# A three-layer graph network on one core: who shares a PSUM bank with whom, and two more blocks of layer 1 by count matrices

## The chip, the cores and the metric

The kernel runs on one core of a Trainium2 chip. Its time is the device time of one launch in microseconds (us), here the median of several runs. The core has five engines with a queue of their own each: TensorE (PE, matrix products, with its weight loads shown as PEld), VectorE (DVE), ScalarE (ACT), GpSimd (POOL) and SyncE (SP, which only issues DMAs here). POOL issues the indirect gathers. Matrix products land in PSUM, which this kernel uses as eight banks of 128 rows by 512 fp32 numbers.

## The reference

`x` has 6250 rows of 256; 100,000 edges `(src, dst)` come sorted by `dst`, and every node has an edge to itself besides. With `dinv = 1/sqrt(degree)`, each of three layers computes

```python
h = h @ W                                     # 256->512, 512->512, 512->256
msg = h[src] * (dinv[src] * dinv[dst])[:, None]
h = relu(segment_sum(msg, dst, n) + b)
```

and the result is `layernorm(x + h)`. The kernel sums neighbours first and multiplies by `W` afterwards in the first two layers, and multiplies by `W3` at the end of layer 2, so that the summed rows are 256, 512 and 256 wide.

## The kernel before

The nodes are 50 blocks of Q = 125 rows. A block's sum over its edges is made in one of two ways.

*Gathered.* The block's edges lie in 16 chunks of 128 places. `gather` (L965) has POOL fetch 128 rows by index into one row buffer of a ring (tiles `room` and `spare`). `more_hots` (L934, DVE) compares column numbers with the edges' destinations and so makes four one-hot matrices `shot`. `product` (L991, PE) multiplies one-hot by rows and adds up in a bank `sacc`. fp32 rows take two passes; most chunks are split first into a high half (L1006, ACT) and a low half (L1009, DVE) in one fp32r tile `halves`, which goes at one pass per half. Chunks of layer 1 are split every other time, those of layer 2 seven times out of eight.

*By a count matrix.* `counts` (L697) makes, for 125 destinations, a matrix of how often each of the 6250 sources occurs: 25 products of one-hot matrices per block (L728, PE, 250 columns each), whose one-hots `hot_lo`, `hot_key` DVE makes by comparison (L705), and which ACT copies as bytes into an SBUF buffer (L737). The matrix is stored to DRAM (`kept`) and fetched back by `fetch`. The sum is then 50 dense products (L1034) with `parts`, the whole table in SBUF, after `converted` (L942, ACT) has turned bytes into fp32r, five products per piece. No gather is needed.

Layer 1 (`layer(0, ...)`) treats blocks 0 to 17 (FEW = 18) by count matrices and gathers 32. Layer 2 is 512 wide: it gathers 44 blocks, and `teams` (L763) does six, three at a time, by streaming the table past stored counts (products L814, one block's share every PACE = 2 chunks) into three further banks. Layer 2 also makes ten further count matrices, one at a time (`alone`). Layer 3 uses all 28 (MANY) and gathers 22.

The order is fixed when the program is built. `layer` walks over the gathered chunks; for each chunk it issues the gather, the splits of earlier chunks, the product of the chunk `lag` = 4 earlier, then the steps of finished blocks (`go`) and the steps of the extras (`go_fixed`): windows, counts, teams. The steps are Python generators that yield the number of chunks to wait (SOON = 2, LATE = 6). All engines work through their queues in that order; semaphores do the rest. `take` and `free` count the holders of a named bank or buffer. In `need`, if no sum bank is free when a block begins, the steps of finished blocks are run without spacing until one is; `late` counts these.

After a block: `after1` scales, transposes into bank `str` (L1057), multiplies by W1 in `smm` (L1081) and stores the rows of table 1. `after2` fetches the block's own rows of table 1 (a row of the gather ring is borrowed for it), waits LATE chunks, adds them (L1102, DVE), gives the sum bank back, scales (L1104, ACT), transposes into `str`, copies out (L1112), and for every two blocks (a couple) multiplies by W2 (L1125) and W3 (L1142), both in bank `win_ps`, and stores table 2.

The eight banks: `near_cols`, three `sacc`, `smm`, `str`, `mat_ps`, `win_ps`. `near_cols` holds the column numbers that every comparison of DVE reads, in its first 250 columns; its other half is the third place for count products in layer 1 (two more lie in `mat_ps`) and the only place in layer 2:

```python
mat_places = [mat_ps[:Q, 0, :G * NB], mat_ps[:Q, 1, :G * NB], near[:Q, 256:256 + G * NB]]
mat_place = mat_places[2 if alone else m % 3]
```

Instructions of different engines on one bank are kept in order by semaphores in this program, whichever columns they touch, and reads against reads as well: before the change, 104 of the copies L737 out of `near_cols` wait for DVE alone.

Of the kernel before, what the change touches and what calls it, by code (L numbers as in the profile page):

```python
# [9 lines left out]
F32 = mybir.dt.float32  # L10
# [11 lines left out]
P = 128  # L22
# [3 lines left out]
Q = 125  # L26
KF = 16
# [13 lines left out]
FEW = 18  # L41
# [5 lines left out]
G = 5  # L47
# [334 lines left out]
def sorted_path(ctx: ExitStack, tc: tile.TileContext, x, edges, starts, found, wts, biases, room, late, out):  # L382
# [43 lines left out]
    mat_ps = ps_mat.tile([P, 2, 256], F32, name="mat_ps")  # L426
# [5 lines left out]
    scratch = w2_sb.rearrange("p k n -> p (k n)")  # L432


    def windows(t):
# [55 lines left out]
        sl_ps = ps_mat.tile([P, 512], F32, name="win_ps")  # L491
# [3 lines left out]
        nc.scalar.copy(slots[:, t], sl_ps.rearrange("p (t v) -> p t v", t=2)[:, :, :Q])  # L495
        yield SOON
# [190 lines left out]
    mat_places = [mat_ps[:Q, 0, :G * NB], mat_ps[:Q, 1, :G * NB], near[:Q, 256:256 + G * NB]]  # L687
# [3 lines left out]
    tr_bank = ps_sum.tile([P, KH, Q], F32, name="str")  # L691
    mat_bank = mat_ps.rearrange("p t n -> p (t n)")
    win_bank = ps_mat.tile([P, HID], F32, name="win_ps")
    idle = {}


    def counts(blocks, places, rush=0, alone=False):  # L697
# [12 lines left out]
        for s in range(total + 5):  # L710
# [10 lines left out]
            if s < total and s % WIDE == 2:  # L721
                t, w = divmod(blocks[s // GB] * GB + s % GB + 1, Q)
                compared(hot[s // WIDE][1][:, 3:], slots[:, t, 1, w:w + WIDE - 3])
            m = s - 4
            if 0 <= m < total:
                hot_lo, hot_key = [h[:, m % WIDE] for h in hot[m // WIDE]]
                mat_place = mat_places[2 if alone else m % 3]
                nc.tensor.matmul(mat_place, lhsT=hot_lo, rhs=hot_key, start=True, stop=True)  # L728
            if alone:
                yield 1  # L730
            else:
                m = s - 5
            if 0 <= m < total:
                n, u = divmod(m, GB)
                place = places[n % len(places)]
                mat_place = mat_places[2 if alone else m % 3]
                nc.scalar.copy(place[:, :, u * G:(u + 1) * G], mat_place.rearrange("p (k r) -> p k r", r=G))  # L737
                if u == GB - 1:
                    by_rows(nc.sync, place.rearrange("p k v -> p (k v)"), kept[blocks[n]], store=True)
                    stored.append(blocks[n])  # L740
            if s >= rush or s % 2:
                yield 1
# [20 lines left out]
    def teams(groups):  # L763
# [35 lines left out]
        for u, (g, k) in enumerate(units):  # L799
# [4 lines left out]
            for n, b in enumerate(groups[g]):  # L804
# [14 lines left out]
                yield PACE  # L819
# [35 lines left out]
    held = {}  # L855

    def free(name, bank=None):
        held[name] -= 1
        if name in idle:
            idle[name].append(bank)  # L860

    team_ended = [None]

    def take(name, most):
        while held.get(name, 0) >= most:
            yield 1
        held[name] = held.get(name, 0) + 1

    def layer(i, width, gathered, dense, after, rows, first=0, spacing=1.0, extras=()):
# [98 lines left out]
        def product(c):  # L968
# [83 lines left out]
    def transposed(z, width, got):  # L1052

        yield from take("tr", 1)
        zt_ps = tr_bank
# [37 lines left out]
    def after2(b, acc, bank):  # L1093
# [19 lines left out]
        free("tr")  # L1113
# [4 lines left out]
        yield soon  # L1118
        yield from take("ht2", 1)
        for f2 in range(0, KH, 2):  # L1120
# [14 lines left out]
            if not f2:  # L1135
                yield soon
# [91 lines left out]
    split = two.enter_context(tc.tile_pool(name="swide_split", bufs=4))  # L1228
    groups = [every[g * TEAM:(g + 1) * TEAM] for g in range(TEAMS)]
# [3 lines left out]
          + [(10 + gap * n, counts([b], (made,), alone=True)) for n, b in enumerate(many[FEW:])])  # L1233
# [190 lines left out]
```

## Time and profile before

| | us |
|---|---|
| median of 3 runs (lowest, highest) | 2312.32 (2309.65, 2316.81) |
| the profiled execution, its own time | 2304.01 |
| its span, first to last instruction | 2302.3 |
| before the first gather | 98 |
| layer 1 to the first gather of layer 2 | 98 to 795 |
| layer 2 to the first gather of layer 3 | 795 to 1832 |
| layer 3 | 1832 to 2302 |

The page gives busy shares per engine over the span; as the three layers have different limits, the times are read by layer. A line of the groups reads: line, engine, operation, output and inputs, shapes, count, busy us, mean ns of one, then the idle time of that engine just before these instructions and what ended it. Waits name who waited for whom, the total, how often, and the longest. In the timeline a matmul's duration includes its way through the array; the distance from one start to the next is what it costs when they come back to back.

### The profile page before, as it was taken

How to read it: one execution, taken by the hardware profiler on the slowest of the kernel's cores; microseconds unless marked ns; L12 is line 12 of the kernel's file. 1: busy time of each engine (PE TensorE's matmuls, PEld its weight loads, DVE VectorE, ACT ScalarE, POOL GpSimd, SP SyncE). 2: the span in 40 equal slices, each digit the busy share in tenths (PEclk: the TensorE clock that was granted, in tenths of full speed). 3: DMA queues.
4: the chain of work that ended last, by engine and by line, in shares of the span. 5: the costliest groups of instructions: out<-in, count | busy, mean ns of one | idle time of the engine just before them, and what ended most of it. 6: DMA issues, size and time to landing. Idle time of an engine off the chain costs nothing.

```text
span 2302.3 us, 30500 instructions
## 1 busy us (share of the span) xinstructions
PE 1977.0 (86%) x8361; PEld 1447.2 (63%) x8361; DVE 1588.9 (69%) x3021; ACT 1340.3 (58%) x2957; POOL 1600.0 (69%) x1620
## 2 busy tenths in 40 slices
PE   3378889899889778989898898899988699999997
PEld 2256666566566445666666666666766577777775
DVE  5677767667664387877776777777777267777776
ACT  1456666656665365766665666566655255555564
POOL 2277677777767577777776777677777177777776
PEclk9989999999999889999999999999999999999998
DMA  8455555665555788888899787888798256667664
GB/s 176 115 146 154 163 168 163 177 182 159 169 164 151 202 246 245 256 261 251 231 256 271 225 266 218 245 234 244 227 276 234 65 162 185 171 183 188 184 175 130
DMA packets 188446, 455.76 MB, mean 198 GB/s; under 512 B 43725, under 2 KB 78682, under 8 KB 188263
## 3 DMA queue, kind: packets, MB, share of 16 engines
q0 software_dynamic: 99776, 301.07, 46.2%
q1 hardware_dynamic: 73367, 140.87, 21.8%
q10 hardware_dynamic: 15120, 11.77, 2.1%
q8 instruction: 67, 1.10, 0.2%
q14 instruction: 116, 0.95, 0.1%
HBM read 399.68 MB, written 53.88 MB: 197 GB/s over the span
## 4 chain that ended last, share of the span: by engine, by line
PE 50%; DVE 16%; DMA 14%; issue 9%; ACT 7%; POOL 2%; ACTq 0%; DVEq 0%; POOLq 0%; SPq 0%
PE sacc L991 16%; DMA room<-tab,ssrc 7%; PE sacc L1034 6%; PE win_ps L1125 4%; DMA spare<-tab,ssrc 4%; PE smm L1034 4%; PE mat_ps L1034 4%; DVE hot_key L705 4%; PE smm L1081 4%; PE win_ps L1034 4%; DVE halves L1009 3%; PE win_ps L1142 2%; ACT halves L1006 2%; DVE shot L934 2%; PE near_cols L728 2%
## 5 line engine op out<-in xcount | busy, mean ns | idle before, releaser
L965 POOL DMA_INDIRECT room<-tab,ssrc x971 | 975.5, 1005 | 329.4 <-issue 144.1
L965 POOL DMA_INDIRECT spare<-tab,ssrc x597 | 589.8, 988 | 198.7 <-issue 85.9
L991 PE MATMUL sacc<-halves,shot 128*125 128x512 f32 x1840 | 685.6, 439 | 24.0 <-DVE halves L1009 20.3
L1009 DVE TENSOR_TENSOR halves<-room,halves 128x512 fp32r<-128x512 f32 (+1 forms) x771 | 430.0, 566 | 254.2 <-ACT halves L1006 250.1
L1006 ACT CAST halves<-room 128x512 fp32r<-128x512 f32 (+1 forms) x771 | 390.0, 520 | 195.1 <-PE sacc L991 86.3
L991 PEld LDWEIGHTS sacc<-halves,shot 128*125 128x125 f32 x1840 | 334.9, 192 | 171.3 <-issue 58.9
L934 DVE TENSOR_TENSOR shot<-near_cols,sdlo 128x500 fp32r<-128x500 f32 x417 | 280.3, 673 | 108.9 <-PE near_cols L728 60.3
L1009 DVE TENSOR_TENSOR halves<-spare,halves 128x256 fp32r<-128x256 f32 (+1 forms) x453 | 241.1, 540 | 149.3 <-ACT halves L1006 143.5
L1034 PE MATMUL sacc<-parts,piece 125*125 125x512 f32 x900 | 333.7, 446 | 3.7 <-ACT piece L942 3.7
L737 ACT CAST room<-near_cols 125x250 uint8<-125x250 f32 x400 | 175.0, 438 | 250.7 <-PE near_cols L728 97.9
L942 ACT CAST piece<-room 125x625 fp32r<-125x625 uint8 x376 | 267.9, 713 | 41.3 <-DVE piece L942 12.4
L1006 ACT CAST halves<-spare 128x256 fp32r<-128x256 f32 (+1 forms) x453 | 222.5, 501 | 98.8 <-PE sacc L991 36.5
L991 PE MATMUL sacc<-room,shot 128*125 128x256 f32 (+1 forms) x596 | 233.5, 475 | 18.1 <-DMA room<-tab,ssrc 13.1
L705 DVE TENSOR_TENSOR hot_key<-near_cols,slots 128x750 bf16<-128x750 f32 (+1 forms) x280 | 223.9, 800 | 19.9 <-ACT room L737 14.6
L728 PE MATMUL near_cols<-hot_key,hot_lo 128*125 128x250 bf16 x400 | 114.6, 287 | 137.9 <-DVE hot_key L705 107.1
L1125 PE MATMUL win_ps<-room,w_sb 128*128 128x250 f32 x800 | 204.1, 380 | 15.8 <-DVE st L1155 11.6
L728 PEld LDWEIGHTS <-hot_lo 128*125 128x125 bf16 x700 | 97.5, 140 | 185.0 <-DVE hot_key L705 133.0
L737 ACT CAST room<-mat_ps 125x250 uint8<-125x250 f32 x300 | 125.5, 437 | 120.6 <-PE mat_ps L728 119.9
L1125 PEld LDWEIGHTS win_ps<-room,w_sb 128*128 128x128 f32 x800 | 152.7, 192 | 53.9 <-DVE st L1155 16.3
L1034 PEld LDWEIGHTS sacc<-parts,piece 125*125 125x125 f32 x900 | 142.1, 190 | 58.9 <-issue 30.5
L1034 PE MATMUL smm<-parts,piece 125*125 125x512 f32 x500 | 141.6, 402 | 5.8 <-ACT piece L942 5.7
L991 PEld LDWEIGHTS sacc<-room,shot 128*125 128x125 f32 x596 | 112.8, 196 | 49.2 <-DMA room<-tab,ssrc 14.0
(201 smaller groups left out, 2637.4 us busy)
## 6 DMA issues: line engine op xcount, KB each, us to landing
room<-kept SPq DMA_DIRECT2D x46, 683.6 KB
parts<-tab SPq DMA_DIRECT2D x55, 448.0 KB
kept<-room SPq DMA_DIRECT2D x28, 683.6 KB
tab<-st SPq DMA_DIRECT2D x71, 224.0 KB
room<-tab,ssrc POOLq DMA_INDIRECT x971
spare<-tab,ssrc POOLq DMA_INDIRECT x597
spare<-tab SPq DMA_DIRECT2D x40, 224.0 KB
out<-st ACTq DMA_DIRECT2D x50, 112.0 KB
```

The source lines that it names most:

```text
L705: nc.vector.tensor_tensor(out, near_cols[:, :shape[2]].unsqueeze(1).to_broadcast(shape), numbers.unsqueeze(2).to_broadcast(shape), op=ALU. ...
L728: nc.tensor.matmul(mat_place, lhsT=hot_lo, rhs=hot_key, start=True, stop=True)
L737: nc.scalar.copy(place[:, :, u * G:(u + 1) * G], mat_place.rearrange("p (k r) -> p k r", r=G))
L934: nc.vector.tensor_tensor(hot[:, :n], near_cols[:, :Q].unsqueeze(1).to_broadcast([P, n, Q]), dlo.rearrange("p b j -> p (b j)")[:, at:at + ...
L942: convert(piece, used[m % 2][:, c * PIECE:(c + 1) * PIECE, :])
L965: nc.gpsimd.indirect_dma_start(out=row, out_offset=None, in_=tables[i], in_offset=bass.IndirectOffsetOnAxis(ap=at, axis=0))
L991: nc.tensor.matmul(acc[:Q, :size], lhsT=hot, rhs=row[:, c0:c0 + size], start=(i == 1 and k == c0 == 0), stop=(k == KF and c0 + size == row ...
L1006: nc.scalar.copy(halves[:, :width], landed[chunk - hi_lag])
L1009: nc.vector.tensor_sub(halves[:, width:], landed.pop(chunk - lo_lag), halves[:, :width].bitcast(F32))
L1034: nc.tensor.matmul(acc_d[:Q], lhsT=got[done // PIECE][:, k % PIECE, :], rhs=parts[:, k], start=False, stop=(k == NB - 1))
L1081: nc.tensor.matmul(y_ps, lhsT=zt[:, k, :], rhs=w1_sb[:, k, :], start=(k == 0), stop=(k == KC - 1))
L1125: nc.tensor.matmul(h_ps[:, f, :], lhsT=w2_sb[:, k, (f2 + f) * P:(f2 + f + 1) * P], rhs=zt2[:, k, :], start=(k == 0), stop=(k == KH - 1))
```

## The change

- FEW is 20: layer 1 makes and uses 20 count matrices and gathers 30 blocks, so 483 gathers in place of 516; layer 2 makes eight count matrices instead of ten.
- `near_cols` is no place for count products any more. In layer 1 they go in pairs, two in the halves of one bank, to whichever of `mat_ps` and `win_ps` is free; in layer 2 to `str`. One copy takes both out, two steps later. The windows (which find the edges for the counts) now take and free `win_ps` explicitly.
- From the 26th product on, layer 1's counts run six products in five chunks.
- In layer 2 the own rows of gathered blocks have a tile `own_row` of their own, fetched five chunks before the block's last product; the add comes SOON chunks after it. The transposes go into the block's own sum bank, which is given back after they are copied out. A team's block waits until it can be the second of a couple, except towards the end.
- The teams run one step in four a chunk earlier.

```diff
-FEW = 18
+FEW = 20
-    mat_ps = ps_mat.tile([P, 2, 256], F32, name="mat_ps")
+    mat_bank = ps_mat.tile([P, HID], F32, name="mat_ps")
+    win_bank = ps_mat.tile([P, HID], F32, name="win_ps")
...
         for h in range(2):
+            yield from take("win", 1)
             c0, c1 = h * half, min(EC, (h + 1) * half)
-            row_ps = ps_mat.tile([P, 512], F32, name="win_ps")
+            row_ps = win_bank
...
+            free("win")
...
-    mat_places = [mat_ps[:Q, 0, :G * NB], mat_ps[:Q, 1, :G * NB], near[:Q, 256:256 + G * NB]]
-    tr_bank = ps_sum.tile([P, KH, Q], F32, name="str")
+    tr_bank = ps_sum.tile([P, HID], F32, name="str")
+    count_banks = {"mat": mat_bank, "win": win_bank, "tr": tr_bank}
-    def counts(blocks, places, rush=0, alone=False):
+    def counts(blocks, places, banks, rush=0):
...
+        def copied(now_on):
+            while full and full[0][0] <= now_on:
+                _, name, ms = full.pop(0)
+                n, u = divmod(ms[0], GB)
+                place = places[n % len(places)]
+                nc.scalar.copy(place[:, :, u * G:(u + len(ms)) * G].rearrange("p k (t r) -> p t k r", r=G),
+                               count_banks[name].rearrange("p (t v) -> p t v", t=2)[:Q, :len(ms), :NB * G]
+                               .rearrange("p t (k r) -> p t k r", r=G))
+                free(name)
...
+            copied(ticks)
             m = s - 4
-            if 0 <= m < total:
+            if 0 <= m:
+                while bank is None:
+                    bank = next((name for name in banks if held.get(name, 0) == 0), None)
+                    if bank is None:
+                        ticks += 1
+                        yield 1
+                        copied(ticks)
+                    else:
+                        held[bank] = 1
                 hot_lo, hot_key = [h[:, m % WIDE] for h in hot[m // WIDE]]
-                mat_place = mat_places[2 if alone else m % 3]
-                nc.tensor.matmul(mat_place, lhsT=hot_lo, rhs=hot_key, start=True, stop=True)
+                nc.tensor.matmul(count_banks[bank][:Q, len(pair) * 256:][:, :G * NB], lhsT=hot_lo, rhs=hot_key,
+                                 start=True, stop=True)
+                pair.append(m)
+                if len(pair) == 2 or m % GB == GB - 1:
+                    full.append((ticks + 2, bank, pair))
+                    bank, pair = None, []
+            if s % 2 if s < rush else s % 6 or not rush:
+                ticks += 1
                 yield 1
...
-                yield PACE
+                yield PACE if (TEAM * u + n) % 4 else PACE - 1
...
-            going.append([chunk + late + min(LATE, most), after(b, acc, bank), most])
+            going.append([chunk + late + min(SOON if i == 1 else LATE, most), after(b, acc, bank), most])
...
+            if i == 1 and j == KF - LATE:
+                by_rows(nc.sync, own_row, tables[1][b * Q:(b + 1) * Q, :])
...
-        own = borrowed(wide_rows[2:], HID)
-        by_rows(nc.sync, own, tables[1][b * Q:(b + 1) * Q, :])
-        yield LATE
+        own = own_row
+        if bank != "acc":
+            own = borrowed(wide_rows[2:], HID)
+            by_rows(nc.sync, own, tables[1][b * Q:(b + 1) * Q, :])
+            yield LATE
         zs = work.tile([Q, HID], F32, name="szs")
         nc.vector.tensor_add(zs, acc[:Q], own)
-        free(bank, acc)
         nc.scalar.activation(zs, zs, AF.Copy, scale=dinv[:, b:b + 1])
         yield soon
-        yield from transposed(zs, HID, got)
-        yield LATE
+        yield from transposed(zs, HID, got, acc)
+        yield soon
+        while bank != "acc" and now < steps(TEAM * TEAMS) - 2 * KF and (len(couple) != 1 or held.get("turn", 0)):
+            yield 1
+        yield from take("turn", 1)
...
         nc.scalar.copy(zt2[:, :, at * Q:(at + 1) * Q], got[0])
-        free("tr")
+        free(bank, acc)
+        free("turn")
...
-    layer(0, C, every[FEW:], few, after1, first_rows, first, spacing, [(0, all_windows()), (1, counts(few, (made, also_made), GB)), (1, fetching_few())])
+    layer(0, C, every[FEW:], few, after1, first_rows, first, spacing, [(0, all_windows()), (1, counts(few, (made, also_made), ("mat", "win"), GB)), (1, fetching_few())])
...
-          + [(10 + gap * n, counts([b], (made,), alone=True)) for n, b in enumerate(many[FEW:])])
+          + [(10 + gap * n, counts([b], (made,), ("tr",))) for n, b in enumerate(many[FEW:])])
```

More of the change, by code (lines that the diff above doesn't have):

```diff
@@ L432, in sorted_path, with free, take @@
     scratch = w2_sb.rearrange("p k n -> p (k n)")
+    held, idle = {}, {}
+    def free(name, bank=None):
+        held[name] -= 1
+        if name in idle:
+            idle[name].append(bank)
+    def take(name, most):
+        while held.get(name, 0) >= most:
+            yield 1
+        held[name] = held.get(name, 0) + 1
     def windows(t):
@@ L490, in windows @@
         yield SOON
-        sl_ps = ps_mat.tile([P, 512], F32, name="win_ps")
+        yield from take("win", 1)
+        sl_ps = win_bank
         nc.tensor.transpose(sl_ps[:, 0:Q], lo, ident[:Q, :Q])
@@ L495, in windows @@
         nc.scalar.copy(slots[:, t], sl_ps.rearrange("p (t v) -> p t v", t=2)[:, :, :Q])
+        free("win")
         yield SOON
@@ L709, in counts @@
         total = len(blocks) * GB
-        for s in range(total + 5):
+        ticks = 0
+        bank, pair, full = None, [], []
+        def copied(now_on):
[7 more added lines that the diff above has]
+                free(name)
+                if u + len(ms) == GB:
+                    by_rows(nc.sync, place.rearrange("p k v -> p (k v)"), kept[blocks[n]], store=True)
+                    stored.append(blocks[n])
+        for s in range(total + 4):
             if s < total and s % GB == 0:
@@ L723, in counts @@
                 compared(hot[s // WIDE][1][:, 3:], slots[:, t, 1, w:w + WIDE - 3])
+            copied(ticks)
             m = s - 4
[L725 to L742 removed]
+            if 0 <= m:
[7 more added lines that the diff above has]
+                        held[bank] = 1
+                hot_lo, hot_key = [h[:, m % WIDE] for h in hot[m // WIDE]]
+                nc.tensor.matmul(count_banks[bank][:Q, len(pair) * 256:][:, :G * NB], lhsT=hot_lo, rhs=hot_key,
[6 more added lines that the diff above has]
+                ticks += 1
+                yield 1
+        while full:
+            ticks += 1
+            yield 1
+            copied(ticks)
     tail = all_parts[:Q, HOME:, :].rearrange("p b c -> p (b c)")
@@ L851, in fetch @@
         there.append(chunk)
[L855 to L860, printed above, removed]
     team_ended = [None]
[L864 to L867, printed above, removed]
     def layer(i, width, gathered, dense, after, rows, first=0, spacing=1.0, extras=()):
@@ L1050, in borrowed, with transposed @@
         return row[:Q, :width]
-    def transposed(z, width, got):
-        yield from take("tr", 1)
-        zt_ps = tr_bank
+    def transposed(z, width, got, bank=None):
+        if bank is None:
+            yield from take("tr", 1)
+            bank = tr_bank
+        zt_ps = bank[:, :KH * Q].rearrange("p (k v) -> p k v", v=Q)
         for k in range(width // P):
@@ L1117, in after2 @@
         couple.clear()
-        yield soon
+        yield SOON
         yield from take("ht2", 1)
@@ L1228, in sorted_path @@
     split = two.enter_context(tc.tile_pool(name="swide_split", bufs=4))
+    own_row = two.enter_context(tc.tile_pool(name="sown_row", bufs=1)).tile([P, HID], F32, name="own_row")[:Q]
     groups = [every[g * TEAM:(g + 1) * TEAM] for g in range(TEAMS)]
```

6 lines of the change are left out of this document (2 added, 4 removed).

## The prediction

> **What bounds the kernel now.** I read the page's shares first. PE is busy 86% of the span, POOL, DVE and DMA 69 to 70%, so no engine is full everywhere, and the layers have to be read apart. The busy time by stage comes next (layers 1, 2, 3; the columns are length, then busy us with counts for PE, PEld, DVE, ACT and POOL, then clock, DMA share, GB/s), and the costliest groups in layer 1 and in layer 2.
>
> ```profile
> 98.00:795.00 697.00, 600.62 (x2572) 418.37 (x2572) 460.92 (x847) 416.56 (x1041) 502.18 (x520) 0.97 0.57 162
> 795.00:1832.00 1037.00, 900.65 (x3747) 658.98 (x3747) 742.89 (x1161) 630.26 (x1255) 731.76 (x710) 0.97 0.83 239
> 1832.00:2302.30 470.30, 443.32 (x1845) 343.70 (x1845) 332.67 (x879) 260.32 (x598) 350.30 (x355) 0.97 0.64 171
> ```
>
> The POOL groups of layer 1 (first line) and of layer 2 show what a gather costs, and the waits of POOL show the smallest gap:
>
> ```profile
> L965 POOL DMA_INDIRECT room<-tab,ssrc x272 | 262.1, 964 | 87.8 <-issue 43.0 <-PE sacc L991 10.1 <-PE sacc L1034 6.1
> ...
> L965 POOL DMA_INDIRECT room<-tab,ssrc x480 | 497.8, 1037 | 174.9 <-issue 78.0 <-PE sacc L991 24.4 <-DVE halves L1009 24.0
> ```
>
> Between two gathers that wait for nothing, POOL's timeline has 0.30 us ("issue"). POOL thus needs 520 x (0.966 + 0.30) = 658 of layer 1's 697 us. Layer 2's 709 gathers run from 795.5 to 1783.1, 988 us; 731.6 busy + 709 x 0.30 = 944 of them are POOL's own pace. The other bound is PE: of its 697 us in layer 1 it idles 96. The groups of count products, first the two of layer 1, then that of layer 2, say for what:
>
> ```profile
> L728 PE MATMUL mat_ps<-hot_key,hot_lo 128*125 128x250 bf16 x300 | 83.4, 281 | 3.0 <-ACT room L737 2.9
> ...
> L728 PE MATMUL near_cols<-hot_key,hot_lo 128*125 128x250 bf16 x150 | 44.2, 295 | 51.0 <-DVE hot_key L705 43.5 <-DVE shot L934 6.2 <-ACT room L737 0.6
> ```
>
> ```profile
> L934 DVE TENSOR_TENSOR shot<-near_cols,sdlo 128x500 fp32r<-128x500 f32 x187 | 125.9, 674 | 72.1 <-PE near_cols L728 44.9 <-ACT room L737 26.5
> L737 ACT CAST room<-near_cols 125x250 uint8<-125x250 f32 x250 | 109.1, 437 | 145.6 <-PE near_cols L728 76.6 <-DVE shot L934 67.6
> L728 PE MATMUL near_cols<-hot_key,hot_lo 128*125 128x250 bf16 x250 | 70.4, 282 | 86.8 <-DVE hot_key L705 63.6 <-ACT room L737 14.0 <-DVE shot L934 8.2
> ```
>
> The same product waits 51.0 us for 150 instructions when it goes to the bank of the column numbers, and 3.0 us for 300 when it goes to `mat_ps`. One-hots are made four steps ahead, so it isn't data that is late: the product waits until DVE has ended its latest comparison, which reads the same bank. In layer 2, where all products go there, it costs PE 86.8 of its 136 idle us, and DVE and ACT wait back.
>
> **The sum**, against the profiled execution's 2304.0 us (the median of the runs is 8.3 above it). PE prices are distances of starts in layer 1:
>
> ```profile
> 738.05 0.40 PE L991 MATMUL sacc<-halves,shot 128*125 128x512 f32 x1
> 738.29 0.59 PE L991 MATMUL sacc<-room,shot 128*125 128x256 f32 x2
> 738.72 1.02 PE L1081 MATMUL smm<-w,szt 128*125 128x512 f32 x2
> ```
>
> A 512-wide product is 0.24 us, an unsplit chunk (two passes) 0.43.
>
> *Layer 1, FEW 18 to 20.* POOL loses 33 gathers: 33 x 1.266 = -41.8 us. PE gains two dense blocks, 2 x 51 x 0.24 = +24.5, loses two gathered ones (each identity + 8 split + 9 unsplit, 9 x 0.24 + 9 x 0.43 = 6.0), -12, and gains 50 count products at 0.13 (the median weight load of this line, 132 ns) to 0.28 each, 7 to 14, I take 10: +22. The bank wait goes: -50. So PE alone would give -28. PE has more to lose: by the written order, blocks find no free sum bank at 43 unspaced steps of layer 1 before, at none after; the waits that such steps make (`smm` on `st` 8.7, `str` on `szt` 6.0, `sacc` on `szs` 4.7) are 19.4 us, which makes PE's own end -28 to -47. The engine that gains less counts, and PE's middle, -37.5, lies just short of POOL's: **-38**, bounds 0 (next part) and -42.
>
> *Dense bursts.* Counts now end just ahead of their use; by the written order most of blocks 3 to 12 issue all 50 dense products at one chunk, 11.9 us. POOL runs on meanwhile: the ring has 25 rows, 32 us. Price 0; if the ring or ACT's ten conversions (7.2 us) held the rest up, the bursts could take what layer 1 gains, which is the 0 above.
>
> *DVE and ACT of layer 1* have room (461 and 417 of 697 us): two more blocks of comparisons are +23 on DVE (208.8 / 18 each). A pair's copy lies between 0.578 us (the nearest row, L1112, 128x500 from PSUM) and 0.874 (two of 437 ns); I take 0.6. 336 pairs and 28 single copies then cost 214 us of ACT in place of 299. Nobody waits for ACT long enough to book that as time.
>
> *Layer 2, the bank.* PE loses 63.6 + 8.2 us of waits and 50 products, -78 to -86. POOL can give back only 988 - 944 = 43 us. Of these some 29 are waits on `sacc` products, 11 on the borrowed row's add, and the rest start-up and landings: I take **-28**, bounds 0 and -43. The 14.0 us that products wait for ACT's copy stay in the sum: one bank is now left, and each pair begins in the step in which the last pair is copied out.
>
> On whether the 944 can fall too, a rule speaks. The page SBUF — State Buffer of the Trainium skill (Who interferes with whom) says that a DVE instruction with two SBUF inputs contends with a GpSimd instruction that reads SBUF, and that one blocks fully. The trace agrees: gathers cost 964 ns in layer 1 and 1037 in layer 2, and nearly all above 1 us overlap a subtraction L1009, two SBUF inputs, 690 ns. By this rule the 616 subtractions keep POOL at 944; were the lengthening only queueing that ends with PE's waits, layer 2 could fall to 709 x (0.95 + 0.30) = 886.
>
> *Own row, banks held.* 44 fetches leave the ring for `own_row`. SP issues each five steps before the block's last product, queued behind table stores for whose data SP often stands (L1155). The add now waits 6.7 + 9.9 us for rows in eight cases; if the single buffer is late, the longest such wait on the chain of waits is 17.4 us. Behind the add stand ACT's scaling L1104 (67.3 us) and then its splits. I take 0, bounds -17 and +17. Transposes no longer queue for `str`; the sum bank is held about eleven steps after the block's end, less than the 16 of the next block, and unspaced steps rise only from 19 to 29 at the change of teams and the end. At the 0.45 us each of layer 1 (19.4 / 43) that is +4.5, inside the rounding of -28.
>
> *Hand-over to layer 3.* POOL stands 48.8 us. PE does three halves of couples there:
>
> ```profile
> 1805.27 3.65 PE L1125 MATMUL win_ps<-room,w_sb 128*128 128x250 f32 x16 [1.70 <-ACT room L1133]
> 1809.59 0.65 PE L1057 MATMUL str<-ident_r,szs 125*128 125x125 f32 x4 [0.67 <-ACT room L1112]
> 1810.31 3.72 PE L1142 MATMUL win_ps<-w,room 128*125 128x256 f32 x16
> 1814.96 3.62 PE L1125 MATMUL win_ps<-room,w_sb 128*128 128x250 f32 x16 [0.93 <-DVE st L1155]
> 1819.56 3.65 PE L1125 MATMUL win_ps<-room,w_sb 128*128 128x250 f32 x16 [0.98 <-ACT room L1133]
> 1824.19 3.72 PE L1142 MATMUL win_ps<-w,room 128*125 128x256 f32 x16 [0.98 <-ACT room L1133]
> ```
>
> By the written order the couple before the last begins at chunk 691 in place of 705 of 709, so about the first ten of these 23 us fall into the layer: **-8**, bounds 0 and -11. *Layer 3* is unchanged: 0.
>
> Sum: -38 - 28 - 8 = -74, which gives 2230 for a profiled execution; with half of the 8.3 us to the median, **2235**.
>
> **Rivals.** *Both layers fall to POOL's pace* (-42, -43, -11 = -96): 2213. For it: layer 3, with PE at 94%, runs at 1.29 us a chunk already. Against it: in layer 1 PE's busy time with the added work, 600.6 + 22, is above POOL's 487 x 1.266 = 617.
>
> *Layer 1 gains nothing*, bursts and the added 22 us of PE eat it: -36, 2273. For it: PE is the fuller engine there (86%). Against: 50 + 19 us of PE's waits there go by name.
>
> *Slower: PE now waits for the copies.* In layer 1 260 pairs begin in one of two banks in about the step in which ACT copies that bank's last pair; before, one or two steps lay between. With w us per pair on PE the whole -74 is gone from 260 w = 74, w = 0.28. At w = 0.4 (the layer-2 row has 14 waits of 1.0 us; that is two pairs in five) it is 104 - 74 = +30: 2339. Against it: ACT waited for PE's product (119.9 us in layer 1) far more than PE for ACT (3.5 us), so ACT is a step ahead.
>
> **How the numbers follow.** The sum's own case 0.58 (2205 to 2262), POOL's pace 0.16, no gain in layer 1 0.15, copies 0.11. The range 2190 to 2290 takes in the first three, bounds included, and leaves out the last. A measurement of this kernel tells about 0.3% (7 us) from no change: faster 0.86, same 0.03, slower 0.11.
>
> **What would show it.** Right: count products wait under 20 us in all for DVE; `shot` has no wait for PE or ACT; layer 1 655 to 665 us long with POOL's gaps near 0.30; layer 2's gathers 955 to 965 us at about 1.03 us busy each; the hand-over near 41 us. Wrong: count products with ACT's copy as releaser above 60 us; gaps of POOL beside the dense bursts; DVE waiting for `own_row`; gathers of layer 2 under 1.0 us.

## The result and the profile after

The changed kernel takes 2346.84 us (median of four runs, 2344.24 to 2350.25) against 2310.99 of the kernel before (2309.13 to 2316.81). The ratio is 1.0152, with a 95% interval of 1.0129 to 1.0175: it is slower by 36 us, where 76 us less were forecast. The profiled execution has a span of 2348.5 us in place of 2302.3.

The changed kernel's busy time by stage (length, then PE, PEld, DVE, ACT, POOL with their counts, then granted clock, DMA share, GB/s), the three layers in the same order as before:

```profile
97.00:877.00 780.00, 648.49 (x2670) 456.22 (x2670) 454.65 (x854) 438.36 (x855) 471.84 (x487) 0.93 0.49 143
877.00:1875.00 998.00, 887.49 (x3697) 653.65 (x3697) 716.50 (x1134) 611.20 (x1110) 741.50 (x709) 0.97 0.85 246
1875.00:2348.50 473.50, 442.78 (x1845) 344.69 (x1845) 333.52 (x879) 260.23 (x598) 352.52 (x355) 0.97 0.64 170
```

Layer 2 is 38 us shorter (1036.4 to 998.2 us between the first gathers of the layers), about as forecast. Layer 1 is 83 us longer (697.4 to 780.1), although POOL has 33 gathers less to do there. PE idles 132 us of it, before 96, and its clock is 0.93 in place of 0.97.

The groups that changed most, first four of layer 1 and then three of layer 2: POOL's gathers, the count products, the comparisons for `shot`, and in layer 1 the dense products:

```profile
L989 POOL DMA_INDIRECT room<-tab,ssrc x252 | 242.4, 962 | 121.6 <-issue 44.5 <-PE sacc L1017 34.5 <-PE mat_ps L766 21.0
L766 PE MATMUL mat_ps<-hot_key,hot_lo 128*125 128x250 bf16 x277 | 72.9, 280 | 17.9 <-ACT room L732 17.5
L958 DVE TENSOR_TENSOR shot<-near_cols,sdlo 128x500 fp32r<-128x500 f32 x128 | 85.6, 669 | 0.6 <-PE sacc L1017 0.5
L1060 PE MATMUL sacc<-parts,piece 125*125 125x512 f32 x1000 | 277.3, 427 | 35.3 <-ACT piece L966 35.2
...
L766 PE MATMUL str<-hot_key,hot_lo 128*125 128x250 bf16 x200 | 55.1, 276 | 64.0 <-ACT room L732 63.8
L958 DVE TENSOR_TENSOR shot<-near_cols,sdlo 128x500 fp32r<-128x500 f32 x187 | 125.1, 669 | 0.0
L989 POOL DMA_INDIRECT room<-tab,ssrc x456 | 479.7, 1052 | 140.1 <-issue 70.5 <-DMA room<-tab,ssrc 26.0 <-DVE halves L1035 18.6
```

The dense products of layer 1 in the kernel before:

```profile
L1034 PE MATMUL sacc<-parts,piece 125*125 125x512 f32 x900 | 333.7, 446 | 3.7 <-ACT piece L942 3.7
```

Count products no longer wait for a comparison, and the comparisons for `shot` wait 0.6 us in all: the bank of the column numbers has its effect. But in layer 1 the dense products now wait 35.2 us for ACT's converted pieces (3.7 us before), and PE products have become releasers of POOL's gathers: beside "issue", which is the fixed 0.30 us, the row names them with 55 us, where before the same row had 16.

In layer 1 POOL's timeline says where. These are the last gathers before one of its pauses and the first after it; a line reads start, duration, instruction, and in brackets the idle time before it and what ended it:

```profile
594.50 0.95 POOL L989 DMA_INDIRECT room<-tab,ssrc  x1 [0.30 <-issue]
595.75 0.95 POOL L989 DMA_INDIRECT room<-tab,ssrc  x1 [0.30 <-issue]
607.54 0.94 POOL L989 DMA_INDIRECT room<-tab,ssrc  x1 [10.84 <-PE mat_ps L766]
608.79 0.95 POOL L989 DMA_INDIRECT room<-tab,ssrc  x1 [0.30 <-issue]
...
639.85 0.94 POOL L989 DMA_INDIRECT room<-tab,ssrc  x1 [7.23 <-PE sacc L1017]
...
675.20 0.94 POOL L989 DMA_INDIRECT room<-tab,ssrc  x1 [7.34 <-PE sacc L1017]
...
710.65 0.94 POOL L989 DMA_INDIRECT spare<-tab,ssrc  x1 [9.65 <-PE sacc L1017]
```

And the timelines of ACT and of PE at the same places:

```profile
592.65 1.94 ACT L966 CAST piece<-room 125x625 fp32r<-125x625 uint8 x3 [3.50 <-DMA room<-kept]
```

```profile
593.42 13.42 PE L1060 MATMUL sacc<-parts,piece 125*125 125x512 f32 x50 [2.35 <-ACT piece L966]
...
626.42 12.72 PE L1060 MATMUL sacc<-parts,piece 125*125 125x512 f32 x47 [3.46 <-ACT piece L966]
```

At 593.4 PE begins all 50 dense products of one block in a row, and for 13.4 us it consumes no gathered row. POOL issues two more gathers, ends at 596.7, 3.3 us after that start, and stands until PE is through. So the ring was nearly full before the burst began. The same picture repeats at later dense blocks, here four times in 115 us, with pauses of 7.2 to 10.8 us.

POOL's 14 pauses of 3 us and more in layer 1 add up to some 118 us; before, there was one of 5.6. Some 19 us of the 118 are steps of the windows, the other 99 lie beside dense blocks. POOL's account of the layer is then: 33 gathers less, -41.8 (33 x 1.266); pauses, +112.4; a longer stand at the end of the layer (41.2 us in place of 17.6), +23.6; the rest, -11.5, is fewer short waits. That is the +82.7. It says where POOL stood; what PE did in that time is told further below.

### The profile page after: what moved, and what is told of

It reads as the page before. It is cut to its first block, busy times and chain, and to the rows that moved or that the text cites. A ratio compares the mean times of both kernels' runs of the same rounds, so it can differ in the third digit from the quotient of the medians.

```text
span 2348.5 us, 30212 instructions
## 1 busy us (share of the span) xinstructions
PE 2011.2 (86%) x8409; PEld 1480.7 (63%) x8409; DVE 1556.8 (66%) x3000; ACT 1342.7 (57%) x2626; POOL 1581.6 (67%) x1587
## 3 DMA queue, kind: packets, MB, share of 16 engines
q1 hardware_dynamic: 73733, 142.43, 21.5%
## 5 line engine op out<-in xcount | busy, mean ns | idle before, releaser
L989 POOL DMA_INDIRECT room<-tab,ssrc x922 | 934.4, 1013 | 326.8 <-issue 142.4
L989 POOL DMA_INDIRECT spare<-tab,ssrc x614 | 613.5, 999 | 249.1 <-issue 104.5
L1035 DVE TENSOR_TENSOR halves<-room,halves 128x512 fp32r<-128x512 f32 (+1 forms) x740 | 410.6, 566 | 371.1 <-ACT halves L1032 365.7
L1032 ACT CAST halves<-room 128x512 fp32r<-128x512 f32 (+1 forms) x740 | 375.5, 520 | 314.4 <-DMA room<-tab,ssrc 197.3
L1035 DVE TENSOR_TENSOR halves<-spare,halves 128x256 fp32r<-128x256 f32 (+1 forms) x468 | 250.8, 545 | 204.4 <-ACT halves L1032 199.5
L966 ACT CAST piece<-room 125x625 fp32r<-125x625 uint8 x396 | 278.3, 713 | 156.7 <-PE sacc L1060 85.9
L1060 PE MATMUL sacc<-parts,piece 125*125 125x512 f32 x1000 | 277.3, 427 | 35.3 <-ACT piece L966 35.2
L1060 PEld LDWEIGHTS sacc<-parts,piece 125*125 125x125 f32 x1000 | 196.1, 203 | 92.9 <-ACT piece L966 39.8
L1017 PE MATMUL sacc<-room,shot 128*125 128x256 f32 (+1 forms) x556 | 214.2, 470 | 16.4 <-DMA room<-tab,ssrc 13.5
L1158 PE MATMUL win_ps<-room,w_sb 128*128 128x250 f32 x800 | 202.8, 380 | 9.8 <-DVE st L1188 5.7
L1158 PEld LDWEIGHTS win_ps<-room,w_sb 128*128 128x128 f32 x800 | 152.8, 192 | 46.7 <-DVE st L1188 10.1
L719 DVE TENSOR_TENSOR hot_lo<-near_cols,slots 128x625 bf16<-128x625 f32 x140 | 112.6, 804 | 79.8 <-PE win_ps L766 41.1
L1109 PE MATMUL smm<-w,szt 128*125 128x512 f32 x200 | 111.7, 643 | 26.7 <-DVE st L1114 25.8
L732 ACT CAST room<-mat_ps 125x500 uint8<-125x500 f32 (+1 forms) x144 | 98.7, 685 | 55.5 <-PE mat_ps L766 54.7
```

Source lines behind the costliest of these rows:

```text
L719: nc.vector.tensor_tensor(out, near_cols[:, :shape[2]].unsqueeze(1).to_broadcast(shape), numbers.unsqueeze(2).to_broadcast(shape), op=ALU. ...
L732: nc.scalar.copy(place[:, :, u * G:(u + len(ms)) * G].rearrange("p k (t r) -> p t k r", r=G), count_banks[name].rearrange("p (t v) -> p t ...
L966: convert(piece, used[m % 2][:, c * PIECE:(c + 1) * PIECE, :])
L989: nc.gpsimd.indirect_dma_start(out=row, out_offset=None, in_=tables[i], in_offset=bass.IndirectOffsetOnAxis(ap=at, axis=0))
L1017: nc.tensor.matmul(acc[:Q, :size], lhsT=hot, rhs=row[:, c0:c0 + size], start=(i == 1 and k == c0 == 0), stop=(k == KF and c0 + size == row ...
L1032: nc.scalar.copy(halves[:, :width], landed[chunk - hi_lag])
```

## The experiments

By the written order of the changed kernel the counts fall behind at the start, where the windows hold `win_ps`. From then on a count block comes out every 21 chunks and is needed every 22, so the delay is hardly made up. Each dense block is overdue when it is fetched (`fetch(b, now + 10)`), and the products owed, 13 in the first and 34 to 50 in all but the first three, are issued at one chunk. In the kernel before, the most at one chunk is under ten.

Theory A, after the result: these bursts fill the ring, and they are the loss; the change of banks is a gain. Theory B: two more dense blocks, or the pairs and their banks, are what PE can't carry. All kernels below do the full computation. Times are medians, ratios are to the kernel before on the same chip; lengths of a layer go from its first gather to that of the next.

### The changed kernel with 18 dense blocks

```diff
-FEW = 20
+FEW = 18
```

> The changed kernel with FEW = 18, so layer 1 makes 18 count matrices and gathers 32 blocks as before, and everything else of the change stays. In the written order no dense block of layer 1 has more than 12 of its 50 products issued at one chunk (in the changed kernel all 20 have 13 to 50). Theory A (the bursts: a dense block that is overdue puts up to 50 products ahead of the gathered chunks in PE's queue, POOL's ring of rows fills, and POOL stands): layer 1 is 655 to 690 us in place of 780, its gaps of 3 us and more on POOL fall from 99 us to under 15, and with layer 2 as in the changed kernel (998) the run is 2225 to 2265. Theory B (PE simply has too much to do in layer 1 with 20 dense blocks): the same direction, so this run does not part A from B. Theory C (PE waits for the pair copies, 29 us in layer 1 of the changed kernel): these waits stay at about 26 us, layer 1 stays above 740, 2310 or more.

Measured: 2250.68 us, ratio 0.9739 (0.9716 to 0.9761). By the written order the counts are then early enough that the largest bursts are two of 11 and 12 products. Layer 1 takes 680.2 us, with no pause of POOL of 3 us, and layer 2 takes 1003.2. So the change of banks, pairs included, is a gain in both layers (-17.2 and -33.2 us against before), and the loss goes with the two blocks. This doesn't yet tell their bursts from their work.

### The changed kernel with its bursts cut to four products a chunk

All 20 blocks and every product stay; a block that is behind issues at most four per chunk.

```diff
                     until = len(dense) * NB
+                elif i == 0:
+                    until = min(until, done + 4)
```

> The changed kernel, FEW = 20, but layer 1 issues at most four dense products per chunk, so that an overdue block is spread over about 12 chunks; the work is the same, only its order changes. Theory A (bursts): layer 1 655 to 690 us, POOL's gaps of 3 us and more under 25 us, the whole 2230 to 2265. Theory B (too much PE work in layer 1): no change, 2335 to 2355, PE as idle as it was. Theory C (copy waits): no change either, 2335 to 2355, with the copy waits still at 25 to 35 us.

Measured: 2259.36 us, ratio 0.9779 (0.975 to 0.9809). The row of its layer 1 by stages, and then the groups of its dense products and of half of POOL's gathers there:

```profile
97.76:785.24 687.48, 611.50 (x2670) 440.42 (x2670) 460.86 (x853) 434.10 (x855) 469.84 (x488) 0.96 0.56 161
```

```profile
L1062 PE MATMUL sacc<-parts,piece 125*125 125x512 f32 x1000 | 305.3, 425 | 12.3 <-ACT piece L966 12.3
L989 POOL DMA_INDIRECT room<-tab,ssrc x252 | 242.5, 962 | 85.7 <-issue 38.7 <-PE sacc L1017 17.2 <-PE win_ps L766 5.5
```

One edit, with the same 1000 dense products and the same late counts, takes 92.6 us out of layer 1 (780.1 to 687.5). POOL's pauses fall from 118 to 11.1 us, PE's wait for pieces from 35.2 to 12.3, and the clock is back at 0.96. The stand of POOL at the end of the layer stays long, 35.7 us. The pairs and the copies are as in the changed kernel, so they are not what costs.

### The changed kernel with its bursts cut to 16

The same line with `done + 16`. A block then needs four chunks, in which PE does little else.

> The changed kernel, FEW = 20, with at most 16 dense products per chunk in layer 1, so an overdue block takes three to four chunks instead of one (50 products, 780 us of layer 1) or about twelve (four per chunk, 687 us). If what counts is how long PE is kept from the gathered chunks, 16 per chunk are still some 4 us of PE per chunk against POOL's 1.27, and layer 1 lies at 735 to 780 us, the whole 2305 to 2350. If it is the single uninterrupted run of 50 products, ten conversions on ACT without anything between, then layer 1 falls to 680 to 700 as with four.

> The kernel of e9_cap16 again, for the same reason. If it counts how long PE is kept from the gathered chunks: layer 1 735 to 780 us, the whole 2305 to 2350. If it is the uninterrupted run of 50: layer 1 680 to 700.

Measured: 0.9898 (0.9796 to 0.9999) on a first chip, of which more below, and 2343.33 us, 1.0149 (1.0107 to 1.0191), on a second: the loss is back. Layer 1 has 775.6 us, 17 pauses with 107.8 us (one of them, 17.5 us, for a step of the windows), and a clock of 0.93. So it is not the single chunk that matters: some 50 dense products, 12 us of PE, with only a few gathered chunks between them cost as much as 50 in a row.

### The kernel before with bursts made on purpose

Old banks, 18 blocks, old pacing; only the dense blocks are fetched 36 chunks after they are stored, so that each is overdue.

```diff
-            fetch(b, now + 10)
+            fetch(b, now + 36)
```

> The kernel before, FEW = 18, where a stored count matrix counts as fetched 36 chunks later instead of 10, so that 18 dense blocks come overdue and 20 to 49 products are issued at one chunk; the work is the same as before. Theory A: POOL stands several us at each block, layer 1 is 730 to 780 us in place of 697 and the whole 2340 to 2390. Theory B and theory C: nothing changes in the work or in the copies, 2300 to 2320.

Measured: 2387.09 us, ratio 1.0329 (1.0305 to 1.0353). Layer 1 takes 778.0 us, 80.6 more than before, with 12 pauses of POOL of 83.7 us in all, 27.8 of them at two steps of the windows. By the written order 18 blocks have bursts of 20 to 49. Two lines of its timelines, PE's and POOL's, and the row of its layer 1:

```profile
465.83 8.96 PE L1034 MATMUL sacc<-parts,piece 125*125 125x512 f32 x30
```

```profile
475.49 0.94 POOL L965 DMA_INDIRECT spare<-tab,ssrc  x1 [6.70 <-PE sacc L991]
```

```profile
96.71:874.67 777.96, 628.44 (x2572) 434.97 (x2572) 458.16 (x847) 423.96 (x1041) 502.29 (x520) 0.93 0.51 145
```

The same instructions in the same numbers as before (2572, 847, 1041, 520), and one number of the plan moved: a loss of the same size comes back without anything else of the change. On PE it shows at another place: PE's wait for the one-hots `hot_key` at the bank of the column numbers is 80.7 us here, 43.5 before. The clock of the layer is 0.93 here too.

### The kernel before with 20 dense blocks and no bursts

Old banks; counts at the new pace, where two or three products at most are owed per chunk.

```diff
-FEW = 18
+FEW = 20
...
-            if s >= rush or s % 2:
+            if s % 2 if s < rush else s % 6 or not rush:
```

> The kernel before with FEW = 20 and its counts at six products in five chunks in layer 1, nothing else; products still go to the bank of the column numbers, and in the written order no chunk has ten dense products or more. Theory A: POOL saves 33 gathers, 42 us, PE gains 22 us of work and keeps its bank waits, so layer 1 is 670 to 705 us (697 before) and the whole 2280 to 2320. Theory B: two dense blocks more cost layer 1 the 83 us of the changed kernel with or without bursts: 2370 or more.

Measured: 2354.51 us, ratio 1.0181 (1.015 to 1.0211): neither theory had it. Layer 1 takes 753.6 us, 56 more than before, with hardly a burst in it. Its PE groups there say what the gathers wait for:

```profile
L1034 PE MATMUL sacc<-parts,piece 125*125 125x512 f32 x1000 | 355.3, 445 | 0.5 <-ACT piece L942 0.5
L728 PE MATMUL near_cols<-hot_key,hot_lo 128*125 128x250 bf16 x166 | 49.2, 296 | 58.2 <-DVE hot_key L705 49.2 <-DVE shot L934 7.3 <-ACT piece L942 0.3
```

Dense products wait for nothing here; the bank waits of the kernel before are there in full (58.2 us, before 51.0). POOL's pauses over 3 us sum to 46.5, 33 of them for steps of the windows; apart from these it stands 1.5 to 3.7 us at a time, spread over the layer, with PE as releaser. So with the old banks two more dense blocks cost something beside their bursts. With the new banks and faster counts they don't (next run). Whether the bank waits make this difference, or the steps of the windows, or the pace of the counts, which differs from that of the kernel before too, no run tells apart; it stays open.

### The changed kernel with faster counts

All of the change stays; its counts run four products in three chunks in place of six in five, so that a block takes some 19 chunks in place of 21 and the counts catch up.

```diff
-            if s % 2 if s < rush else s % 6 or not rush:
+            if s % 2 if s < rush else s % 4 or not rush:
```

> The changed kernel, FEW = 20, with one number changed: from the 26th product on layer 1 makes four count products in three chunks instead of six in five, so the count matrices are stored ahead of their use (the 20th at chunk 415 instead of 453 of 483), and in the written order only three of the 20 dense blocks issue 10 to 17 products at one chunk, the others two or three. Theory A (overdue dense blocks make bursts): layer 1 665 to 700 us in place of 780, without the 36 us hand-over of the capped run (16 to 24 us), the whole 2230 to 2260. Theory D (the copies of the pairs are what holds PE; more of them per chunk makes it worse): layer 1 780 or more, 2345 or more.

> The kernel of e6_rate4 again, since its chip ran the kernel before at 2817 us instead of 2310 and at a clock of 0.90, where sizes can't be compared with the other runs. At a time of before near 2310, theory A (overdue dense blocks make bursts): layer 1 665 to 700 us in place of 780, a hand-over of 16 to 24 us, the whole 2230 to 2260. Theory D (the copies of the pairs hold PE): layer 1 780 or more, 2345 or more.

Measured: 0.9511 (0.9435 to 0.9588) on the first chip; on the second 2207.56 us, ratio 0.9566 (0.9538 to 0.9594). It is the fastest kernel of this study, 139 us below the changed one by one number of its pacing, and below what theory A expected of it, in layer 1 (643.4 us) and as a whole. The first chip ran everything slower, the kernel before at 2816.53 us, so these four kernels were run again on another. By the written order three bursts of 10 to 17 products are left. Layer 1, by its whole length and by stretches of 100 us:

```profile
96.42:739.81 643.39, 596.55 (x2670) 436.13 (x2670) 460.04 (x853) 429.38 (x855) 472.69 (x488) 0.98 0.61 173
300.00:400.00 100.00, 97.99 (x456) 72.23 (x455) 77.91 (x145) 74.00 (x148) 75.76 (x80) 1.00 0.65 186
400.00:500.00 100.00, 98.33 (x453) 71.83 (x453) 78.05 (x145) 73.51 (x147) 75.24 (x78) 1.00 0.62 174
500.00:600.00 100.00, 99.26 (x470) 73.91 (x469) 79.97 (x139) 77.41 (x154) 75.94 (x80) 1.00 0.66 188
600.00:700.00 100.00, 100.00 (x442) 74.60 (x441) 57.84 (x108) 67.38 (x136) 75.92 (x80) 1.00 0.61 174
```

The same stretches of the changed kernel:

```profile
300.00:400.00 100.00, 86.17 (x363) 60.30 (x362) 56.89 (x113) 56.71 (x112) 64.50 (x67) 0.95 0.48 136
400.00:500.00 100.00, 85.26 (x350) 60.08 (x348) 54.98 (x99) 58.42 (x113) 55.87 (x60) 0.91 0.48 138
500.00:600.00 100.00, 83.44 (x335) 57.79 (x336) 57.00 (x102) 56.02 (x111) 60.31 (x63) 0.91 0.51 150
```

POOL issues 78 to 80 gathers in 100 us, one each 1.25 to 1.28 us, which is its own pace (1.266); in the changed kernel it is 60 to 67. PE is full as well. With dense work spread over the chunks both engines run at their ends at once, and layer 1 is 137 us shorter than in the changed kernel, 54 shorter than before.

### The same with 19 dense blocks

```diff
-FEW = 20
+FEW = 19
```

> The same with FEW = 19: 19 blocks of layer 1 by count matrices, 31 gathered, nine count matrices left for layer 2. If a block more by counts saves its 20 us of gathers while PE still keeps up, the run lies between the one with 18 (2250.7) and the one with 20, within 10 us of both: 2235 to 2260. If PE is the bound at 20 and POOL at 18, 19 is the fastest of the three.

> The kernel of e7_rate4_few19 again, for the same reason. Within 10 us of the runs with 18 (2250.7) and with 20: 2235 to 2260; the fastest of the three if PE is the bound at 20 and POOL at 18.

Measured: 0.9581 (0.9506 to 0.9655) on the first chip; on the second 2223.05 us, 0.963 (0.9601 to 0.9659). That is below the range that was expected, and 19 is not the fastest of the three: 20 is. Layer 1 has 659.9 us, 16.5 more than with 20 blocks. It issues 500 gathers in place of 483, and 17 gathers at 1.266 are 21.5 us, so at the faster pace a dense block in place of a gathered one is worth most of its gathers.

### The change with 18 blocks, and layer 2's counts back in the old bank

Here layer 2's count products go, one at a time, to the free half of `near_cols`, and the rest is as in the changed kernel with 18 blocks.

```diff
-FEW = 20
+FEW = 18
-          + [(10 + gap * n, counts([b], (made,), ("tr",))) for n, b in enumerate(many[FEW:])])
+          + [(10 + gap * n, counts([b], (made,), ("near",))) for n, b in enumerate(many[FEW:])])
```

> The changed kernel with FEW = 18, where the count products of layer 2 go back, one at a time, into the second half of the bank of the column numbers; layer 1, the own rows, the transposes and the couples stay as changed. Theory A2 (layer 2's gain is the bank alone): layer 2's gathers take 985 to 990 us again (969 with FEW = 18 and the count products elsewhere), PE's waits at the count products 70 us or more, and the whole 2264 to 2275. Theory E (layer 2's gain is the own row and the ring row that no longer is borrowed): the gathers stay at 965 to 972 us and the whole at 2247 to 2256. In both the hand-over to layer 3 stays at 33 to 35 us.

> The kernel of e8_near_layer2 again, for the same reason. Theory A2 (layer 2's gain in its gathers is the bank alone): 985 to 990 us for them, PE's waits at the count products 70 us or more, the whole 2264 to 2275. Theory E (the gain is the own row and the ring row that is no longer borrowed): 965 to 972 us, the whole 2247 to 2256. Hand-over to layer 3 33 to 35 us in both.

Measured: 0.9721 (0.9649 to 0.9792) on the first chip; on the second 2272.55 us, 0.9841 (0.9814 to 0.9868), some 22 us above the changed kernel with 18 blocks, from which it differs in the bank (and the pairs) of these ten count matrices alone. Its comparisons and products in layer 2:

```profile
L958 DVE TENSOR_TENSOR shot<-near_cols,sdlo 128x500 fp32r<-128x500 f32 x187 | 125.9, 674 | 76.4 <-PE near_cols L766 76.4
L766 PE MATMUL near_cols<-hot_key,hot_lo 128*125 128x250 bf16 x250 | 68.1, 272 | 101.5 <-ACT room L732 93.1 <-DVE shot L958 7.5
```

DVE's waits at the shared bank are back (76.4 us), and layer 2's gathers take 997.8 us in place of 968.9, more than theory A2 expected. PE's 101.5 us are another matter: 93.1 of them are for ACT's copy, and the run with `str` has 56.3 of that kind too, for half as many copies. In the kernel before that wait was 14.0 us, with the copy at another place in the written order, and its gathers took 987.6 us, 10 less than here. So 29 us of layer 2's gathers are the bank's and the pairs' together, and no run parts the two. The hand-over to layer 3 stays short, 33.5 us here and 34.4 there: its gain belongs to the rest of the change (own rows, transposes, couples, teams), which no run took apart.

## Why the prediction was wrong

*Layer 1* was forecast 38 us shorter and is 83 us longer. The term that failed is that of the *Dense bursts*: "POOL runs on meanwhile: the ring has 25 rows, 32 us. Price 0". The bursts were foreseen about as they are. What was wrong is the price of 0. The 25 rows cover 32 us only if they are free when the burst comes. At 593.4 some 23 of them were taken: POOL got two more gathers out. Counted from the starts of the gathers and the ends of the instructions that read their rows, 17 to 24 rows are taken at any time from 390 to 830 us; with faster counts it is 5 to 14 from 310 to 710 us, though PE is full there. (The kernel before has up to 24 too, but no bursts.) On POOL's side the price was 12 pauses of together 99 us. The bound of this term, that it could take what layer 1 gains, was too small: the layer lost 83 us beside the 38 that it was to gain. The kernel before with bursts (+80.6 us in layer 1) and the changed one without (-92.6) show from both sides that the bursts are the loss.

Nor would a ring with room have made the bursts free, as far as the trace tells. PE is not short of rows: its list of waits in layer 1 has no wait for a gathered row. The largest beside those for count copies and windows are these (total, times, longest, in us). Below them stand the busy times in the burst at 593.4 and between it and the next one (length, then PE, PEld, DVE, ACT, POOL):

```profile
PE sacc L1060 <- ACT piece L966: 35.2, 12, 5.3
PE smm L1109 <- DVE st L1114: 25.4, 14, 6.7
PE str L1085 <- ACT szt L1103: 13.7, 7, 4.0
PE sacc L1017 <- DVE halves L1035: 11.2, 22, 1.3
```

```profile
593.00:607.00 14.00, 13.58 (x52) 10.86 (x53) 2.49 (x5) 8.06 (x14) 2.84 (x3) 0.88 0.16 47
607.00:626.00 19.00, 15.18 (x73) 9.82 (x71) 17.44 (x31) 12.19 (x27) 14.18 (x15) 1.00 0.69 199
```

ACT works through its queue in order. It first stands for the late matrix itself (the pieces wait 35.3 us for `kept`), and then converts the pieces of the burst in step with PE, one each 1.16 us. Its splits come behind them, so DVE stands 12.67 us for one. DVE is busy for 2.49 of the 14 us of the burst and for 17.44 of the 19 behind it, where it makes up for this, and there PE's other products wait for it and for ACT. The prediction named this road ("ACT's ten conversions (7.2 us) held the rest up") and bounded it, like the ring, by the layer's gain alone. The 19.4 us of waits (`smm` on `st`, `str` on `szt`, `sacc` on `szs`) that the sum let PE lose became 39.7 us; with faster counts they are 7.8. For the same 2670 products of layer 1 PE idles 85 us more than with faster counts and is busy 52 us more, which makes up the 137 us between the two. What a larger ring alone, or more piece buffers, would give, no run shows.

At the end of the layer PE was a ring behind POOL, so that the hand-over took 41.2 us in place of 17.6. It is 35.7 with the bursts cut to four, so this part is PE's lag and not the single burst; in the run with faster counts it is 16.4.

*The price of two more blocks*, without bursts, was too careful where the banks are new: layer 1 is 54 us shorter with faster counts, where -38 was taken and -42 was the bound. The sum priced the 33 gathers at POOL's own 1.266, but before they cost 1.317 each (679.8 / 516), with POOL's waits for PE: that is 43.5 us, and the 483 that are left cost 1.298 (627.0 / 483), 9 us less in all; the rest is the hand-over. The terms don't add as the sum had it, though: the banks with 18 blocks are worth 17 us, two more blocks at the faster pace 37 more, and two more blocks with the old banks cost 56.

*Layer 2, the bank*: forecast -28, with POOL's own pace as the end. The gathers took 964.8 in place of 987.6 us, -23, and the run with the old bank puts 29 us on it. POOL's pace stayed the end: 741.5 us busy for 709 gathers, 1.046 each, and 0.30 between them are 954 of the 965. The rule of the Trainium skill (SBUF — State Buffer, Who interferes with whom), by which a DVE instruction with two SBUF inputs contends with a GpSimd instruction that reads SBUF, had spoken for that. The trace agrees: in layer 2 of the changed kernel 190 gathers take more than 1 us, and 186 of them overlap a subtraction L1035. But 390 more overlap one and are not lengthened, so an overlap alone does not do it.

*Own row, banks held*: forecast 0; no run isolates it. The add waits 2.1 us for `own_row` in all, where it waited 16.9 for rows before, so the single buffer was not late. *Hand-over to layer 3*: forecast -8 with -11 as its end, measured -15.4 (48.8 to 33.4). PE does two halves of couples (L1158) and one product with W3 (L1175) after the last rows, where it did three and two before. *Layer 3*: forecast 0, measured +2.5.

*The rival of the copies*, by which PE would wait for ACT's copies, had 60 us of such waits as its mark, and that mark was met: 28.9 us in layer 1 and 63.8 in layer 2. A pair's copy also took 0.70 to 0.71 us, where 0.6 was taken. It isn't the cause. The run with faster counts has 21.1 and 58.4 of the same waits and is 139 us faster in all. In layer 2 they took the place of 86.8 us of bank waits, and POOL bounds that layer; in layer 1 they are 0.11 us for each of 260 pairs, where the rival needed 0.28. The mark that counted was the other one, "gaps of POOL beside the dense bursts".

## What to carry to other kernels

A buffer between two engines hides a burst only by what is free in it when the burst comes; where the consumer lags, the buffer stands full, and each burst of the consumer's other work is a pause of the producer. The pause shows the loss and need not be its cause: look at what the consumer itself waits for, and at which engines stand in order behind the burst. Before a change that alters when work becomes ready, count from the written order how much of it is issued at one place, and spread what is overdue. Two engines that are both near their limit can run at it together, as the version with faster counts shows, when each step carries the same mixture.

## What the runs showed of the hardware

The granted clock falls after PE has waited, and a burst begins at the low clock. The changed kernel before and in the burst at 593.4 (the value before the last two columns is the clock):

```profile
590.00:593.40 3.40, 1.06 (x5) 0.43 (x3) 1.84 (x4) 0.75 (x2) 2.49 (x4) 1.00 0.94 294
593.40:597.00 3.60, 3.58 (x9) 2.85 (x10) 0.00 (x0) 1.91 (x3) 2.70 (x3) 0.53 0.41 118
597.00:600.00 3.00, 3.00 (x15) 2.39 (x14) 0.00 (x0) 1.45 (x3) 0.00 (x0) 1.00 0.17 44
600.00:607.00 7.00, 7.00 (x32) 5.62 (x31) 2.49 (x5) 4.31 (x8) 0.00 (x0) 1.00 0.00 1
```

In the 3.4 us before the burst PE is busy for 1.06, as it waits for the late matrix. Then come 3.6 us at 0.53 with nine products, and the rest of the burst runs at 1.00, fifteen products in 3.0 us. The trace's clock records have 17 such drops between 160 and 830 us, and before each one PE was busy at most 52% of 3.4 us. With faster counts PE is 98 to 100% busy for 400 us, and there is no drop between 160 and 700 us. So the clock follows PE's waits, and the bursts lower it by the waits that they bring. All three kernels with large bursts have 0.93 over layer 1, the others 0.95 to 0.98. From 160 to 830 us the clock of the changed kernel is 0.94 in the mean, by which some 40 of the 670 us would be lost if PE was full in all drops (an estimate from these two numbers): the smaller part of the 137 between it and the run with faster counts.

A whole chip can be slower than another: the kernel before took 2816.53 us on one and 2306.75 to 2310.99 on the rest, and layer 3, with the same instructions, 597 in place of 470 us. The ratios of the four kernels run on both kept their order, but three of them gained 0.5 to 1.2 per cent more on the slow chip, and the kernel cut to 16 products was a gain of 1.0 per cent there and a loss of 1.5 here. The clock was 0.88 to 0.91 there in place of 0.94 to 0.97, too little for the 27% of layer 3. Single instructions took as long on both (in layer 3 of the run with faster counts ACT's conversions L966 711 ns on each, gathers 969 and 990 ns); the engines stood longer between them, and why is open.
